# Moving the choice of the next image's tokens behind the present image's feed-forward, and splitting 165 kept tokens 83 + 82 instead of 128 + 37

## The chip, the cores and the metric

The kernel runs on one core of a Trainium2 chip. The metric is the device time of one execution in microseconds (us). Before the change it is 12924.97 us, the median of three runs (12904.25 to 12950.39). The profile is of one more execution, which took 12889.47 us.

A core has five engines, each working through its own queue of instructions: TensorE (PE in the profile: matrix products; PEld: its weight loads), VectorE (DVE), ScalarE (ACT), GpSimd (POOL), and SyncE (SP), which here only starts DMA transfers.

## The reference, cut to what matters

64 images of 256 x 256 pass a tokenizer of four Fourier layers. The 256 rows of its output and 77 text tokens make 333 tokens of width 256 for each image. One layer follows, image by image, and the change lies in it:

```
h = concat([tokenizer(x), txt], axis=1)          # [64, 333, 256]
h = h + attention(layernorm(h))                  # one head, softmax over 333 tokens
z = layernorm(h)
weights = z @ wr + br                            # one number for each token
sel = the 165 tokens of largest weight, in order # k = 166 by top_k, the last one dropped
y = (gelu(z[sel] @ w1 + b1) @ w2 + b2) * weights[sel]
out = h + z;  out[sel] += y
```

All arithmetic is in float32.

## The kernel before, in words

The first three quarters of the time go to the tokenizer, whose order is written out by hand (a `manual_schedule` block) and which the change doesn't touch. The last stage, from about 9950 us on, handles the 64 images one after the other. Its program order is a loop over the images (L1038 to L1046), but the framework's scheduler decides at build time in which order each engine's queue gets the instructions: among those that are ready by its own estimate it prefers the one that comes first in the program. Once built, each queue is fixed, and semaphores make an instruction wait for what it needs.

Four functions make up an image's work.

- `image_rows(b)` (L809 to L838) makes the last tokenizer step. DVE forms two small products (L813, L817), PE multiplies them (L819), DVE copies the result (`y`, through L163), and PE starts a sum in the PSUM tile `hp` with it (L824). Then come eight pieces `ch` of 1 MB, loaded by SP (L829, five buffers), each with four matmuls (L831). Each of these matmuls appears twice in the profile, so a piece is 8 PE instructions and an image has 64. ACT moves the finished `hp` into `h` (L836), and SP loads the text rows (L837).
- `attention(h)` (L903 to L966) is a layer norm (`layer_norm`, L840: statistics L845 and L846 on DVE, root L848 on ACT, reciprocal L849, normalised rows `az` by L853), transposition by PE (L863) with copies of `azT`, the queries (L909), scores (L921), their maximum (L926) and exponential (L928), the values (L935), the transposed probabilities (L950), the product (L959) and the residual sum `h1` (L962). A second layer norm gives `z` (its tile is `fz`). At the end it called `select(z)`.
- `select(z)` (L867 to L901) finds the kept tokens. DVE takes the weight of each token (L875) and puts it on a diagonal (`dg`, L879), one such matrix for each group of 128, 128 and 77 tokens; PE turns the three into a row of all weights in every partition (L880); DVE moves it out (L882), and then counts by comparisons how many tokens beat each one (L889, L893, L895, L898). The count gives the factor `fw` (L899) and the 0/1 matrix `place` (L900), which maps tokens to kept places.
- `feed_forward(b, h1, z, fw, place)` (L970 to L1036) gathers the kept tokens by a product with `place` (L977, copied to `zs`), transposes `place` in two pieces for the way back (L988, copied to `back`), applies the two layers (L994, gelu on ACT at L998, L1005, bias L1009 to `yT`), transposes the result in the same two pieces (L1015, copied to `ys`), scatters it by a product (L1024, two pieces for each group of tokens), and adds it to the rest (L1027). SP stores the result in 17 transfers (L1032, L1036). POOL adds `z` to `h1` (L1020) and the output bias to `h` (L955).

`evict` (L157) copies alternate between DVE (L163) and ACT (L161).

In the loop, iteration `b` does `image_rows(b + 2)`, then `attention(b + 1)` with its `select`, then `feed_forward(b)`. So the choice for image `b + 1` stood ahead of the feed-forward of image `b`, whose own choice had been made one iteration earlier. In the built queues the PE order for one image was: L909, L921, L935, L950, L959 with one piece of L831 inside it, two pieces of L831, L880, L977, L988, L994, L1005, L1015, L1024, L819, L863, L824, five pieces of L831. In this order L880 and L977 are interleaved.

Of the kernel before, what the change touches and what calls it, by code (L numbers as in the profile page):

```python
# [25 lines left out]
KEPT = max(1, int(0.5 * TOK)) - 1  # L26
# [96 lines left out]
def tile_fno_fusion_transformer(ctx: ExitStack, tc: tile.TileContext, a, cst_d, grid_d, out):  # L123
    nc = tc.nc
    x = a["x"].rearrange("b x y o -> b x (y o)")
    B = x.shape[0]
# [30 lines left out]
    def evict(dst, src, act_every=3):  # L157

        flip[0] += 1
        if act_every and flip[0] % act_every == 0:  # L160
            nc.scalar.copy(dst, src)  # L161
        else:
            nc.vector.tensor_copy(dst, src)  # L163
# [642 lines left out]
    def psum():  # L806
        return pp.tile([128, 512], F32, name="pp")
# [32 lines left out]
    def layer_norm(h, name):  # L840
        mv = small.tile([128, 3, 2], F32, name=f"{name}mv")
        nc.vector.memset(mv, 1.0)
        for t in range(3):
            bs = small.tile([128, 6], F32, name=f"{name}bs")
            nc.vector.bn_stats(bs[:rows[t]], h[:rows[t], t, :])  # L845
            nc.vector.bn_aggr(mv[:rows[t], t, :], bs[:rows[t]])  # L846
        rs = small.tile([128, 3], F32, name=f"{name}rs")
        nc.scalar.activation(rs, mv[:, :, 1], AF.Sqrt, bias=epsc, scale=1.0)  # L848
        nc.vector.reciprocal(rs, rs)  # L849
        z = tp.tile([128, 3, D], F32, name=f"{name}z")  # L850
        for t in range(3):
            r = rows[t]
            nc.vector.tensor_scalar(  # L853
                z[:r, t, :], h[:r, t, :], mv[:r, t, 0:1], rs[:r, t:t + 1], ALU.subtract, ALU.mult
            )
        if name == "f":
            return z
        zT = tp.tile([128, 2, TOK], F32, name=f"{name}zT")
        for dh in range(2):
            ps = psum()  # L860
            for t in range(3):
                r = rows[t]
                nc.tensor.transpose(ps[:, toks[t]], z[:r, t, 128 * dh:128 * dh + 128], ID[:r, :r])  # L863
            evict(zT[:, dh, :], ps[:, :TOK], 2)
        return z, zT

    def select(z):  # L867


        wcol = small.tile([128, 3], F32, name="wcol")  # L870
        ps = psum()
        for t in range(3):
            r = rows[t]
            junk = tp.tile([128, TOK], F32, name="junk")
            nc.vector.scalar_tensor_tensor(  # L875
                junk[:r, :D], z[:r, t, :], 1.0, wrB[:r], ALU.mult, ALU.mult, accum_out=wcol[:r, t:t + 1]
            )
            dg = tp.tile([128, 128], F32, name="dg")
            nc.vector.tensor_scalar(dg[:r, :r], ID[:r, :r], wcol[:r, t:t + 1], None, ALU.mult)  # L879
            nc.tensor.matmul(ps[:, toks[t]], lhsT=ONES[:r], rhs=dg[:r, :r], start=True, stop=True)  # L880
        wrow = tp.tile([128, TOK], F32, name="wrow")
        nc.vector.tensor_scalar(wrow, ps[:, :TOK], brB, None, ALU.add)  # L882
        fw = small.tile([128, 3], F32, name="fw")
        place = tp.tile([128, 3, KEPT], F32, name="place")
        for t in range(3):
            r = rows[t]
            junk = tp.tile([128, TOK], F32, name="junk")
            wc = small.tile([128, 1], F32, name="wc")
            nc.vector.scalar_tensor_tensor(  # L889
                junk[:r, :r], wrow[:r, toks[t]], 1.0, ID[:r, :r], ALU.mult, ALU.mult, accum_out=wc[:r]  # L890
            )
            gt = small.tile([128, 1], F32, name="gt")
            nc.vector.tensor_scalar(junk[:r], wrow[:r], wc[:r], None, ALU.is_gt, ALU.add, accum_out=gt[:r])  # L893
            eq = small.tile([128, 1], F32, name="eq")
            nc.vector.scalar_tensor_tensor(  # L895
                junk[:r], wrow[:r], wc[:r], TRI[:r, t, :], ALU.is_equal, ALU.mult, accum_out=eq[:r]
            )
            nc.vector.tensor_add(gt[:r], gt[:r], eq[:r])  # L898
            nc.vector.tensor_scalar(fw[:r, t:t + 1], gt[:r], float(KEPT), wc[:r], ALU.is_lt, ALU.mult)  # L899
            nc.vector.tensor_scalar(place[:r, t, :], IOTA[:r], gt[:r], None, ALU.is_equal)  # L900
        return fw, place  # L901

    def attention(h):  # L903
        z, zT = layer_norm(h, "a")
        qT = tp.tile([128, 2, TOK], F32, name="qT")
        for eh in range(2):
            ps = psum()
            for dh in range(2):
                nc.tensor.matmul(  # L909
                    ps[:, :TOK], lhsT=wqk[:, dh, 128 * eh:128 * eh + 128], rhs=zT[:, dh, :],  # L910
                    start=dh == 0, stop=dh == 1,
                )
            nc.scalar.activation(qT[:, eh, :], ps[:, :TOK], AF.Identity, bias=bqk[:, eh:eh + 1], scale=1.0)
        v = tp.tile([128, 3, D + 2], F32, name="v")
        p_ = tp.tile([128, 3, TOK], F32, name="prob")
        sm = small.tile([128, 3], F32, name="sm")
        for t in range(3):
            r = rows[t]
            ps = psum()
            for eh in range(2):  # L920
                nc.tensor.matmul(  # L921
                    ps[:r, :TOK], lhsT=qT[:, eh, toks[t]], rhs=zT[:, eh, :], start=eh == 0, stop=eh == 1
                )
            scale = 1.0 / D ** 0.5
            mx = small.tile([128, 1], F32, name="mx")
            nc.vector.reduce_max(mx[:r], ps[:r, :TOK], axis=AX.X)  # L926
            nc.vector.tensor_scalar_mul(mx[:r], mx[:r], -scale)
            nc.scalar.activation(  # L928
                p_[:r, t, :], ps[:r, :TOK], AF.Exp, bias=mx[:r], scale=scale, accum_out=sm[:r, t:t + 1]
            )  # L930
        for t in range(3):
            r = rows[t]
            ps = psum()
            for dh in range(2):
                nc.tensor.matmul(  # L935
                    ps[:r, :D + 2], lhsT=zT[:, dh, toks[t]], rhs=wvE[:, dh, :], start=dh == 0, stop=dh == 1
                )
            nc.vector.tensor_add(v[:r, t, :], ps[:r, :D + 2], bvE[:r])
            nc.vector.reciprocal(sm[:r, t:t + 1], sm[:r, t:t + 1])

            for n in range(2):
                nz = small.tile([128, 1], F32, name="nz")
                nc.vector.tensor_scalar(nz[:r], v[:r, t, D + n:D + n + 1], 0.0, None, ALU.not_equal)
                nc.vector.tensor_mul(sm[:r, t:t + 1], sm[:r, t:t + 1], nz[:r])
        pT = tp.tile([128, 3, TOK], F32, name="probT")
        for jt in range(3):
            r = rows[jt]
            ps = psum()
            for t in range(3):
                nc.tensor.transpose(ps[:r, toks[t]], p_[:rows[t], t, toks[jt]], ID[:rows[t], :rows[t]])  # L950
            evict(pT[:r, jt, :], ps[:r, :TOK], 2)
        h1 = tp.tile([128, 3, D], F32, name="h1")
        for t in range(3):
            r = rows[t]
            nc.gpsimd.tensor_add(h[:r, t, :], h[:r, t, :], boB[:r])  # L955
            ps = psum()
            for jt in range(3):
                rj = rows[jt]
                nc.tensor.matmul(  # L959
                    ps[:r, :D], lhsT=pT[:rj, jt, toks[t]], rhs=v[:rj, jt, 0:D], start=jt == 0, stop=jt == 2  # L960
                )
            nc.vector.scalar_tensor_tensor(  # L962
                h1[:r, t, :], ps[:r, :D], sm[:r, t:t + 1], h[:r, t, :], ALU.mult, ALU.add
            )
        z = layer_norm(h1, "f")
        return (h1, z) + select(z)  # L966

    kept = [slice(0, 128), slice(128, KEPT)]

    def feed_forward(b, h1, z, fw, place):  # L970

# [65 lines left out]

    hs = {n: image_rows(n) for n in range(min(2, B))}  # L1038
    done = attention(hs.pop(0))
    for b in range(B):  # L1040
        now = done
        if b + 2 < B:
            hs[b + 2] = image_rows(b + 2)
        if b + 1 < B:
            done = attention(hs.pop(b + 1))
        feed_forward(b, *now)  # L1046


# [31 lines left out]
```

## Time and profile before

| | |
|---|---|
| runs | 12904.25, 12924.97, 12950.39 us |
| profiled execution | 12889.47 us, span 12887.7 us |
| busy share of the span | PE 89%, PEld 47%, DVE 68%, ACT 47%, POOL 9% |
| last stage (9950 to 12888 us) | 2938 us; PE busy 2657.59 us, DVE 1714.61, ACT 1040.41, POOL 322.02 |
| last stage, TensorE clock granted | 0.97 |
| last stage, DMA | 196 GB/s, share 0.53 |

A group line of the profile names line, engine, operation, the tile written and the tiles read, the shape (partitions x elements), the count, the busy time, the mean of one in ns, and after the second bar the time for which the engine was idle just before these instructions and what ended it. In the chain of waits each line is a start, a duration and the instruction or wait that the end of the program hung on at that moment. "PEclk" is the share of full clock that TensorE was granted. [...]durations of successive matmuls overlap; what one costs in a run is the distance of the starts.

### The profile page before, as it was taken

Reading aid. Unit: us, or ns where it says so; the run is one execution under the profiler, and the core shown is the slowest. Engines: PE = TensorE matmul, PEld = TensorE weight load, DVE = VectorE, ACT = ScalarE, POOL = GpSimd, SP = SyncE. Lnnn points to the kernel's source line nnn. Section 1 sums busy time; section 2 is a strip of 40 time slices with the busy share of each in tenths; the row PEclk is TensorE's granted clock in tenths of the full one; section 3 lists DMA queues with packets and bytes.
Section 4 is the critical chain, followed back from the end, with each engine's and each line's share of the span. In section 5 each row is a group of like instructions: output and inputs, shape, how many; then the busy total and the mean of one; then the engine's idle time right before and its main releaser. Section 6 shows DMA issues by size and latency. Waiting matters only on the chain.

```text
span 12887.7 us, 406626 instructions
## 1 busy us (share of the span) xinstructions
PE 11449.8 (89%) x182458; PEld 6025.9 (47%) x182458; DVE 8775.7 (68%) x10606; ACT 6088.1 (47%) x10114; POOL 1110.9 (9%) x1183
## 2 busy tenths in 40 slices
PE   7799999999699999999969999999996899999998
PEld 5344444444344444444434444444443566666666
DVE  2777777777677777777767777776775556665555
ACT  2455555555355555555545555555553333333333
POOL 2100000000200000000020000000002111111111
PEclk9899999999899999999989999999997999999999
DMA  4555555555888889899989998988898555555553
GB/s 116 199 202 200 202 204 200 202 203 201 288 344 345 349 347 353 346 353 352 352 295 349 352 352 346 349 346 345 343 348 281 193 202 209 207 197 197 200 206 138
DMA packets 571125, 3484.57 MB, mean 270 GB/s; under 512 B 78224, under 2 KB 129248, under 8 KB 172448
## 3 DMA queue, kind: packets, MB, share of 16 engines
q1 hardware_dynamic: 565376, 3454.84, 71.0%
q8 instruction: 1428, 23.40, 0.7%
q0 software_dynamic: 4000, 3.71, 0.1%
q14 instruction: 321, 2.63, 0.1%
HBM read 1761.32 MB, written 1696.92 MB: 268 GB/s over the span
## 4 chain that ended last, share of the span: by engine, by line
PE 69%; DVE 16%; issue 7%; DMA 4%; ACT 3%; POOL 1%; SPq 0%; DVEq 0%; ACTq 0%; POOLq 0%
PE ring L607 14%; PE ring L624 13%; PE ring L572 11%; PE ring L583 7%; PE ring L647 4%; PE hp L831 3%; DVE t L595 3%; DVE vo L591 2%; DVE zt L634 2%; PE pp L959 2%; PE pp L994 2%; PE pp L1024 2%; PE pp L921 2%; PE pp L935 1%; PE pp L909 1%
## 5 line engine op out<-in xcount | busy, mean ns | idle before, releaser
L614 ACT ACTIVATE ring<-ring 128x1024 f32<-128x1024 f32 x3072 | 3108.9, 1012 | 1194.7 <-PE ring L607 1159.3
L595 DVE STREAM_TRANSPOSE t<-vo 128x2048 f32<-128x2048 f32 x1536 | 3550.1, 2311 | 173.5 <-ACT vo L590 12.6
L607 PE MATMUL ring<-vo,w 32*32 32x512 f32 x49152 | 2849.6, 624 | 391.2 <-DVE zt L634 139.6
L590 ACT ACTIVATE vo<-ring 128x1024 f32<-128x1024 f32 x1536 | 1568.2, 1021 | 3012.4 <-PE ring L583 2363.1
L591 DVE TENSOR_SCALAR vo<-ring 128x1024 f32<-128x1024 f32 x1536 | 1858.2, 1210 | 612.1 <-PE ring L583 424.5
L624 PE MATMUL ring<-t,cst 32*32 32x512 f32 x49152 | 1862.7, 602 | 288.5 <-issue 288.5
L634 DVE STREAM_TRANSPOSE zt<-ring 128x1024 f32<-128x1024 f32 x384 | 712.0, 1926 | 1630.5 <-PE ring L624 1630.5
L607 PEld LDWEIGHTS ring<-vo,w 32*32 32x32 f32 x49152 | 761.8, 105 | 1899.6 <-ACT ring L614 482.3
L624 PEld LDWEIGHTS ring<-t,cst 32*32 32x32 f32 x49152 | 981.1, 103 | 1132.1 <-issue 674.5
L583 PE MATMUL ring<-vin,ws 32*32 32x512 f32 x32768 | 1240.2, 608 | 19.9 <-issue 17.4
L542 POOL TENSOR_TENSOR ams<-am,sk 48x512 f32<-48x512 f32 x384 | 486.9, 1268 | 8439.5 <-DMA am<-mix 8005.8
L647 PEld LDWEIGHTS ring<-cst,zt 128*128 128x128 f32 x4608 | 533.2, 193 | 174.9 <-ACT vo L590 162.6
L614 ACT ACTIVATION_READ_ACCUMULATOR ring<-ring 128x1 f32 x3072 | 584.2, 190 | 0.0
L647 PE MATMUL ring<-cst,zt 128*128 128x96 f32 x4608 | 565.3, 279 | 9.2 <-DVE zt L634 9.2
L831 PE MATMUL hp<-ch,win 128*32 128x512 f32 x4096 | 487.1, 604 | 5.1 <-DMA ch<-v 5.1
L553 PE MATMUL ring<-ams,cst 49*128 49x512 f32 (+1 forms) x1536 | 392.4, 620 | 59.5 <-POOL ams L542 49.1
L583 PEld LDWEIGHTS ring<-vin,ws 32*32 32x32 f32 x32768 | 253.4, 103 | 402.6 <-issue 369.7
L926 DVE TENSOR_REDUCE mx<-pp 128x1 f32<-128x333 f32 (+1 forms) x192 | 96.6, 503 | 457.4 <-PE pp L921 453.9
L1020 POOL TENSOR_TENSOR h<-h,fz 128x256 f32<-128x256 f32 (+1 forms) x192 | 182.5, 975 | 1886.6 <-DVE fz L853 1886.6
L1005 PE MATMUL pp<-g,w 128*128 128x165 f32 x2048 | 314.8, 306 | 9.2 <-ACT g L998 3.6
L994 PE MATMUL pp<-zs,w 128*128 128x165 f32 x2048 | 305.4, 307 | 3.3 <-DVE zs L163 3.3
L1005 PEld LDWEIGHTS pp<-g,w 128*128 128x128 f32 x2048 | 292.2, 189 | 24.4 <-ACT g L998 24.4
(955 smaller groups left out, 11982.8 us busy)
## 6 DMA issues: line engine op xcount, KB each, us to landing
v<-vo SPq DMA_DIRECT2D x1536, 1024.0 KB
vin<-v SPq DMA_DIRECT2D x1024, 1024.0 KB
ch<-v SPq DMA_DIRECT2D x512, 1024.0 KB
mix<-ob SPq DMA_DIRECT2D x192, 256.0 KB
am<-mix SPq DMA_DIRECT2D x384, 96.0 KB
xin<-in_x_dram SPq DMA_DIRECT2D x64, 256.0 KB
mv<-in_x_dram SPq DMA_DIRECT2D x256, 64.0 KB
out_dram<-o SPq DMA_DIRECT2D x1024, 16.0 KB
```

The source lines that it names most:

```text
L572: nc.tensor.matmul(ps[n][:, 256 * r:256 * r + 256], lhsT=y_[b][32 * n:32 * n + K, t // 4, q:q + 4, :].rearrange("p q c -> p (q c)"), rhs=m ...
L583: nc.tensor.matmul(ps[n][32 * j:32 * j + 32], lhsT=ws[32 * n:32 * n + 32], rhs=v[32 * n:32 * n + 32, 2 * j:2 * j + 2, :], start=False, sto ...
L590: nc.scalar.activation(of[:, 0:2], t2[0], AF.Relu)
L591: nc.vector.tensor_scalar(of[:, 2:4], t2[1], 0.0, None, ALU.max)
L595: nc.vector.transpose(t32[b, t // 2][:, :, 8 * (t % 2):8 * (t % 2) + 8, :].rearrange("p y s c -> p s y c"), o.rearrange("p s (y l) -> p s ...
L607: nc.tensor.matmul(ps[n][32 * j:32 * j + 32], lhsT=w4[i + 1][32 * n:32 * n + 32], rhs=o[32 * n:32 * n + 32, 2 * j:2 * j + 2, :], start=Tru ...
L614: nc.scalar.activation(t2[n], t2[n], AF.Square, accum_out=acc[:, at:at + 1])
L624: nc.tensor.matmul(ps[n][32 * j:32 * j + 32], lhsT=FYT[32 * n:32 * n + 32, k, :], rhs=t32[b, j][32 * n:32 * n + 32, k].rearrange("p s c -> ...
L634: nc.vector.transpose(zt[:, h].rearrange("p k c -> p c k"), t2[h].rearrange("p n (s c) -> p c (n s)", c=C),)
L647: nc.tensor.matmul(ps[:, 0, 96 * g:96 * g + 96], lhsT=zt[:, h, k0:k0 + 4, :].rearrange("p k c -> p (k c)"), rhs=FX[:, h, 48 * r:48 * r + 9 ...
L831: nc.tensor.matmul(hp[32 * g:32 * g + 32], lhsT=win[:, 7 - t:39 - t], rhs=ch[:, g], start=False, stop=t == 7, skip_group_check=True,)
L1005: nc.tensor.matmul(ps[:, :KEPT], lhsT=w2[:, hb, 128 * dh:128 * dh + 128], rhs=g[:, hb, :], start=hb == 0, stop=hb == HID // 128 - 1,)
```

## The change

The call of `select` leaves `attention` and is put behind `feed_forward(b)` in the loop, so that the choice for image `b + 1` comes after the feed-forward of image `b` in program order, and ahead of `image_rows(b + 3)` and `attention(b + 2)`. For the first image it follows `attention(0)`. The two pieces in which kept tokens are transposed and scattered are 83 and 82 long instead of 128 and 37.

```diff
         z = layer_norm(h1, "f")
-        return (h1, z) + select(z)
+        return h1, z
 
-    kept = [slice(0, 128), slice(128, KEPT)]
+    kept = [slice(0, (KEPT + 1) // 2), slice((KEPT + 1) // 2, KEPT)]
...
     done = attention(hs.pop(0))
+    done += select(done[1])
     for b in range(B):
         now = done
         if b + 2 < B:
             hs[b + 2] = image_rows(b + 2)
         if b + 1 < B:
             done = attention(hs.pop(b + 1))
         feed_forward(b, *now)
+        if b + 1 < B:
+            done += select(done[1])
```

Built, the changed program has these queues in the last stage (the order of instructions is fixed before any run; line numbers are those of the kernel before, which differ by three or less). On PE, L880 stands after L1024, in one group of two and one later, around L819; L977 follows L959. The pieces of L831 are no longer in three runs for each image: in the first nine images there are three to five runs, and from then on six or seven, between the instructions of L959, L977, L988, L994 and L1005, with the last two or three pieces after L824. On ACT the eight gelus (L998) of an image stand together, and the root for the next image's `az` comes after the copy of `ys`; table loads ahead of L998 fall from 124 to 66. On DVE, L813 and L817 for a later image now stand ahead of the copy of `ys` or of L1027. The layer norm rows `az` of the next image stand ahead of the comparisons of `select` in 36 images, and behind nearly all of them (behind the last L895) in 26 images: every second one from the eleventh on.

## The prediction

> **What bounds the kernel now.** I read the busy times by stage first, then the waits of PE in the last stage, then the chain of waits through one image, then PE's and DVE's timelines of that image. The stages:
>
> ```profile
> 0.00:9950.00 9950.00, 8792.24 (x167162) 4253.60 (x167162) 7061.08 (x4408) 5047.66 (x8073) 788.91 (x799) 0.96 0.78 292
> 9950.00:12888.00 2938.00, 2657.59 (x15296) 1772.29 (x15296) 1714.61 (x6199) 1040.41 (x2041) 322.02 (x384) 0.97 0.53 196
> ```
>
> The columns are the stretch, its length, the busy times of PE, PEld, DVE, ACT and POOL, PE's clock, the DMA share and GB/s. Only the second line can change. PE is busy for 90% of it (DVE 58%), so it is PE's queue, and the 280 us in which PE stands, that count. PE's waits in this stage:
>
> ```profile
> PE pp L880 <- DVE dg L879: 197.3, 64, 7.6
> PE pp L1024 <- DVE ys L163: 25.3, 62, 0.4
> PE pp L1015 <- ACT yT L1009: 17.4, 64, 0.3
> ...
> PE pp L1005 <- ACT g L998: 3.6, 24, 0.2
> ```
>
> One wait dominates: `select`'s first matmul waits for its diagonal, 197.3 us over 64 images. The chain of waits through one image shows why:
>
> ```profile
> 11000.10 1.94 PE pp L959 x8
> ...
> 11002.14 0.49 DVE h L962
> 11002.66 0.43 DVE fbs L845
> ...
> 11003.87 1.46 DVE fz L853 x3
> 11005.33 0.69 DVE junk L875 x4
> 11006.02 1.35 DVE dg L879 x2
> ...
> 11007.42 0.49 PE pp L880 x2
> ```
>
> From the last product of attention to L880 runs a ladder over DVE and ACT (second layer norm, weights, diagonal), 5.4 us long. PE fills part with two pieces of L831 and stands for 2.94 us (each image repeats after 44.32 us). The feed-forward behind it (L977) needs none of this: its own choice is an iteration old.
>
> [...]the clock is halved. Here even the 2.94 us gap sometimes does it:
>
> ```profile
> 10555.07:10561.89 6.82, 5.93 (x24) 5.74 (x25) 5.67 (x23) 0.30 (x1) 1.34 (x2) 0.50 0.70 265
> 10602.85:10606.27 3.42, 3.42 (x13) 3.25 (x14) 2.28 (x8) 0.00 (x0) 0.39 (x1) 0.50 1.03 400
> ```
>
> That pair comes once in eight images (358 us) and makes two of them 46.85 and 45.65 us long instead of 44.32: 3.9 us. [...]L853 on 77 rows takes 808 ns beside POOL's L955, on 128 rows 409 ns.[...]
>
> **The change part by part**, on the profiled execution (12889.47 us). Which queue gets what is read from the built program; durations from the trace.
>
> 1. *L880 leaves the place between L959 and L977.* L977 can start when L959 ends. The 197.3 us go, but for a few at the first and last image: -193. What is late next is in 3 to 5.
>
> 2. *The gelus stay together.* Before, the next image's root (L848) parted them with two table loads of 1.28 us. 58 loads go, 74 us of ACT. PE waited only 3.6 us for gelu, because L1005 had other blocks to multiply: -3.
>
> 3. *L831 is cut into more runs.* Each run of these 32-column matmuls has a price, from PE's timeline:
>
> ```profile
> 10993.09 2.78 PE L935 MATMUL pp<-wvE,azT 128*128 128x258 f32 x12
> ...
> 10996.68 2.43 PE L959 MATMUL pp<-v,probT 128*128 128x256 f32 x10
> 10999.04 1.07 PE L831 MATMUL hp<-ch,win 128*32 128x512 f32 x8
> 11000.03 2.00 PE L959 MATMUL pp<-v,probT 77*128 77x256 f32 x8
> 11001.96 0.64 PE L831 MATMUL hp<-ch,win 128*32 128x512 f32 x4
> ```
>
> By the starts, one piece alone takes 0.99 us; in the run of five it took 4.43 / 5 = 0.89, so 0.10 more. L959's 18 instructions take 2.36 + 1.93 = 4.29 us; at L935's undisturbed pace (2.61 / 12 = 0.2175) they would take 3.92. That 0.37 belongs to two entries and two exits, some 0.2 a run. So a run costs about 0.3 to 0.33. From 3 runs to 6 or 7 in 52 images, and one more in the first nine: (52 x 3.5 + 9) x 0.33 = +63. Between the narrower products of the feed-forward the edges may hide; the run's own lengthening is the least. Bounds +19 (0.10) and +63; I take +63, as every edge in the trace pays.
>
> 4. *The comparisons of `select` now stand on DVE behind the feed-forward; in 26 images ahead of the next `az`*, whose transposition (L863) PE needs next. From the last L1024: L880 (twice two instructions) and L819 take PE 1.2 us, the copy `y` 0.4, so L882 starts at 1.7. From L882 to the end of the last L895 the trace has 11008.75 to 13.83, less 0.24 for a copy between: 4.8, so 6.5. The reciprocal (0.18), three L853 (1.47 beside POOL) and the L898 to L900 between them (0.5): 8.7. The last L863 and the copy of `azT`: 9.5. Until then PE has L880 1.0, L819 0.55, L824 1.06, two pieces of L831 1.85, L863 0.73: 5.2. It waits 4.3, and 0.4 more for `y` at L824 and for a second `azT` copy: 26 x 4.7 = +122. Before, `az` was done 7 us before L1024 ended. Bounds 3[...] and 6: +78 to +156.
>
> In the other 36 images `az` comes first. There the comparisons lie beside L909 and L921 and end before L926 is due (4.2 us after L909 starts): nothing. `place` itself is due at L977, over 15 us later: nothing.
>
> 5. *In 27 of these 36, `ys` is late.* DVE has the `az` statistics, L813 and L817 ahead of the copy `ys`, and they wait for L836, that is for the last piece of L831. After it: 0.15 and 0.69 (L836), then L845 three times at 0.32, L813 1.12, L846 0.1, L817 1.83 by the distances of starts: 4.9. PE meanwhile has 20 to 22 instructions of L1005 at 0.14, 3.0, and then 0.85 to `ys` (11019.92 to 11020.77): 3.85. Late by 1.0: 27 x 1.0 = +27, bounds 0 and +55.
>
> 6. *The clock.* From the last L831 to L909 there are some 5.5 us with only 0.7 of transpositions in them, which can halve the clock oftener than 2.94 us did. The shortest half-clock record is 3.41 us[...]: I take 0.45, so 12 of 26 at 3.9 us, +45, and the old eight pairs go, -31: +14. Bounds -31 and +70.
>
> 7. *83 + 82.* The same number of instructions, moving the same columns: L988 of 128 and of 37 columns takes 290 and 289 ns, L1024 with 128 and 37 rows 431 and 429; copies of 37 and 128 rows cost by their 333 columns (ACT 431 ns). 0, bounds ±4 for the weight loads (151 and 123 ns, hidden under the matmuls).
>
> 8. *DMA.* L829 and the 17 stores keep their order around L1027. After the stores five buffers are free and 5 MB arrive in about 13 us (11032 to 11045 at some 420 GB/s), while the first of these pieces is due 20 us after L1024. With `ch` waits of 5.1 us in the whole stage: 0, bounds 0 and +15.
>
> Sum: -193 - 3 + 63 + 122 + 27 + 14 = **+30 us**: 12919 on the profiled execution, which lies 0.3% under the median; on the median **12955**. A measurement here can tell about 0.3% (39 us) from no change.
>
> **The rivals.**
>
> - *Slower, by a half-clock trap.* At L863 PE nearly stands for 5.5 us in every second image. If each of these gaps, rather than a third to a half, halves the clock, 26 x 3.9 = 101 replaces the old 31: +70 instead of +14; with the wait at 5.3 instead of 4.7, +16 more: 13027. It decides from the point where the clock record shows 0.5 after most of these gaps. For it: 2.94 us were enough at times. Against: eight in sixty.
> - *Faster, since the new waits are smaller than read.* Edges of L831 hidden beside products of 165 columns (+19), a wait of 3.5 at L863 (+91), `ys` in time (+5), no half clock from the old gap (-10): -193 - 3 + 19 + 91 + 5 - 10 = -91, so 12834. For it: DVE and ACT have 40% and more of slack. Against: the edges are in every case of the trace, and the order on DVE is fixed.
> - *It doesn't do what it says.* That L880 still stands in PE's way could only be if the queue were not as built; the wait would merely move to L977 (for `place`). That is 15 us early: no chance given.
>
> **How the numbers follow.** The forecast's case has a chance of 0.46; by its own spread (bounds of 3 to 5 mostly, about ±30) 0.29 of that is within 0.3%, 0.15 above, 0.02 below. The slower rival has 0.30, of which 0.27 above. The faster rival has 0.24, of which 0.19 below. Slower 0.42, within 0.3% 0.37, faster 0.21. The range leaves a tenth on each side: from 12865, short of the faster rival's own time, to 13035, past the slower rival's. The likeliest case alone holds 12925 to 12990.
>
> **What would show it.** Step 1: no wait L880 <- DVE `dg` of more than some us in all, and L977 straight behind L959. Step 3: PE's starts around single pieces of L831 between L994 and L1005 show 0.3 us a run. Step 4: a wait of PE at L863 for `az` and L909 for `azT` of 110 to 130 us in all, in every second image, with L895 just before `az` on DVE. Step 5: L1024 <- `ys` at about 50 us instead of 25.3. Step 6: the clock at 0.5 behind these gaps. The forecast is wrong if L863 hardly waits, or if the images alternate by 44 and 49 us rather than 44 to 46.

## The result, and the profile after

The changed kernel takes 12849.98 us (median of 4 runs, 12845.12 to 12878.92); the kernel before, on the same chip, 12933.66 (4 runs, 12904.25 to 12950.39). The ratio is 0.9942 (95% interval 0.9918 to 0.9967): faster by 0.6%, where the forecast was 0.2% slower with a range that began at 12865 us. The profiled execution took 12849.86 us (span 12848.1), 39.6 less than that of before. So about half of the gain between the medians is seen between the two profiles; the profile of before lay 44 us under the median of these runs, that of after on its median. Two executions in the experiments, one of the kernel before (18084 us, clock 0.78) and one of e5 (22392 us, clock 0.51), were in a slow state and are left out of every comparison.

The last stage by its busy times (stretch, length, PE, PEld, DVE, ACT, POOL, PE's clock, DMA share, GB/s), and PE's longest waits in it (total us, times, longest):

```profile
9950.00:12849.00 2899.00, 2693.06 (x15296) 1785.46 (x15296) 1705.51 (x6199) 984.68 (x1984) 326.11 (x384) 0.96 0.55 198
```

```profile
PE pp L863 <- DVE az L853: 78.5, 52, 2.7
PE pp L1024 <- DVE ys L163: 46.0, 61, 1.6
PE pp L909 <- ACT azT L161: 19.6, 41, 0.5
PE pp L1015 <- ACT yT L1009: 18.1, 64, 1.0
PE pp L880 <- DVE dg L879: 9.8, 13, 7.6
```

The wait at L880 has gone from 197.3 to 9.8 us, and new waits have come at L863, L909 and for `ys`. All of PE's waits over 0.15 us together fall by 70 us, from 265.6 to 195.3, yet PE is busy for 36 us longer, at a clock of 0.96 instead of 0.97. PE's timeline shows the cost of the single pieces of L831 between the products of the feed-forward (start, duration, group, idle time before):

```profile
11005.88 1.06 PE L831 MATMUL hp<-ch,win 128*32 128x512 f32 x8
11006.88 2.51 PE L994 MATMUL pp<-zs,w 128*128 128x165 f32 x16
11009.32 1.06 PE L831 MATMUL hp<-ch,win 128*32 128x512 f32 x8
```

Sixteen L994 take 2.44 us from start to start of the next group, 0.15 each with the edge, against 0.14 in the unbroken run of before (4.54 / 32); each piece takes 1.00, where a piece of a run of five takes 0.89 on average.

What the forecast did not have is L1024. Before:

```profile
11021.25 3.75 PE L1024 MATMUL pp<-ys,back 128*128 128x256 f32 x12 [0.41 <-DVE ys L163]
11024.94 0.62 PE L819 MATMUL pp<-cstt,a 48*32 48x256 f32 x2
```

and after:

```profile
10970.34 2.87 PE L1024 MATMUL pp<-ys,back 83*128 83x256 f32 x12 [0.40 <-DVE ys L163]
10973.04 0.61 PE L880 MATMUL pp<-dg,cst 128*128 128x128 f32 x4
```

From its start to that of the next group the same twelve instructions take 3.69 us before and 2.70 after; over all images at full clock 3.681 and 2.705. That is 0.976 us an image, 62.5 us in all.

### The profile page after: what moved, and what is told of

It is laid out like the page before. It is cut to its first block, busy times and chain, and to the rows that moved or that the text cites. A ratio compares the mean times of both kernels' runs of the same rounds, so it can differ in the third digit from the quotient of the medians.

```text
span 12848.1 us, 406325 instructions
## 1 busy us (share of the span) xinstructions
PE 11486.4 (89%) x182458; PEld 6038.9 (47%) x182458; DVE 8768.3 (68%) x10606; ACT 6032.7 (47%) x10057; POOL 1115.6 (9%) x1183
## 4 chain that ended last, share of the span: by engine, by line
PE 70%; DVE 17%; issue 7%; DMA 4%; ACT 1%; POOL 1%; SPq 0%; DVEq 0%; ACTq 0%; POOLq 0%
PE ring L607 14%; PE ring L624 13%; PE ring L572 11%; PE ring L583 7%; PE ring L647 4%; PE hp L831 3%; DVE t L595 3%; DVE vo L591 3%; PE pp L994 2%; DVE zt L634 2%; PE pp L959 2%; PE pp L921 2%; PE pp L909 2%; PE pp L1005 1%; PE pp L935 1%
## 5 line engine op out<-in xcount | busy, mean ns | idle before, releaser
L583 PE MATMUL ring<-vin,ws 32*32 32x512 f32 x32768 | 1235.7, 606 | 25.1 <-issue 20.7
L831 PE MATMUL hp<-ch,win 128*32 128x512 f32 x4096 | 533.6, 615 | 5.0 <-DMA ch<-v 5.0
L845 DVE BATCH_NORM_STATS2 abs<-h 128x6 f32<-128x256 f32 (+1 forms) x192 | 75.9, 402 | 439.3 <-ACT h L836 419.1
L994 PEld LDWEIGHTS pp<-zs,w 128*128 128x128 f32 x2048 | 291.2, 190 | 99.2 <-issue 68.8
L994 PE MATMUL pp<-zs,w 128*128 128x165 f32 x2048 | 332.1, 310 | 0.0
L1005 PEld LDWEIGHTS pp<-g,w 128*128 128x128 f32 x2048 | 292.5, 189 | 73.6 <-issue 68.8
L1005 PE MATMUL pp<-g,w 128*128 128x165 f32 x2048 | 321.5, 307 | 0.1
```

The costliest lines, as they stand in the source:

```text
L583: nc.tensor.matmul(ps[n][32 * j:32 * j + 32], lhsT=ws[32 * n:32 * n + 32], rhs=v[32 * n:32 * n + 32, 2 * j:2 * j + 2, :], start=False, sto ...
L831: nc.tensor.matmul(hp[32 * g:32 * g + 32], lhsT=win[:, 7 - t:39 - t], rhs=ch[:, g], start=False, stop=t == 7, skip_group_check=True,)
L994: nc.tensor.matmul(ps[:, :KEPT], lhsT=w1[:, dh, 128 * hb:128 * hb + 128], rhs=zs[:, dh, :], start=dh == 0, stop=dh == 1,)
```

## The experiments

Each ratio is to the kernel before, measured beside it on the same chip; its median was then 12899 to 12928 us. "Half-clock time" is the sum of the stretches with 0.5 in the clock record of the profiled execution that begin after 9950 us; nearly the same number follows from the stage's PEclk, as 2 x (1 - PEclk) x length. An "undisturbed image" is the distance from one image's first L909 to the next where no such stretch lies between. Where a kernel has lines inserted, its line numbers behind them are one to three higher: L1025 to L1027 are then the scatter product that is L1024 before.

### One part at a time: e1 to e4

**e1: before, with pieces of 83 and 82.**

```diff
-    kept = [slice(0, 128), slice(128, KEPT)]
+    kept = [slice(0, (KEPT + 1) // 2), slice((KEPT + 1) // 2, KEPT)]
```

> The kernel before with the pieces of 83 and 82 alone; the choice of tokens stays where it was. Theory A (the pieces brought the gain: in L1024, weights of 128 rows and of 37 rows alternated, and each change between them kept the next weight load from being done ahead): L1024 takes 2.70 us for an image instead of 3.68, so 62 us faster, ratio 0.995, and PE's wait at L880 stays at about 197 us. Theory B (the move brought the gain, as the split costs and saves nothing): ratio 1.000, L1024 at 3.68 us.

Measured: 12916.62 us, 1.0003 (0.9993 to 1.0012). The ratio is that of theory B, and yet theory B does not hold: L1024 takes 2.797 us an image here, 0.884 less than before, and no gain comes of it.

**e2: the kernel after, with pieces of 128 and 37** (the same line, the other way).

> The choice of tokens moved behind the feed-forward, the pieces left at 128 and 37. Theory A: L1024 at 3.68 us for an image; the move alone costs +23 us by the two profiles (12848.1 - 12887.7 + 62.5), ratio 1.002, or up to 20 us less than before if the execution profiled before was a low one: 0.998 to 1.003. Theory B: the whole measured gain, ratio 0.994.

Measured: 13048.33 us, 1.0101 (1.0084 to 1.0117): slower by 1%. Both theories miss.

**e3: before, with pieces of 101 and 64** (`slice(0, 101), slice(101, KEPT)`).

> The kernel before with pieces of 101 and 64. Theory A1 ([...]the change of kind costs): L1024 stays near 3.68 us, ratio 1.000. Theory A2 (the 37-row operand was dear by its being short or by the unevenness of the two): L1024 falls by more than half of the 0.98 us, ratio about 0.997.

Measured: 12925.22 us, 1.0009 (0.9997 to 1.002). L1024 takes 3.681 us, exactly as with 128 and 37: with 64 rows in the smaller piece it is as dear as with 37.

**e4: before, 128 and 37, with the loop over the pieces outermost in L1024**, so that the kind of piece changes once instead of five times. It needs three PSUM tiles at a time.

```diff
-            ps = psum()
-            for c, k in enumerate(kept):
-                n = k.stop - k.start
+        pss = [psum() for t in range(3)]
+        for c, k in enumerate(kept):
+            n = k.stop - k.start
+            for t in range(3):
+                r = rows[t]
                 nc.tensor.matmul(
...
+        for t in range(3):
+            r = rows[t]
```

> The kernel before, pieces 128 and 37, but in the scatter product all three token groups of the first piece come first and then all three of the second (three PSUM tiles open at once)[...]. Theory A (alternation costs): L1024 at about 2.8 us, ratio 0.995 to 0.996; DVE's L1027 come later by about 1.3 us, and what of that PE sees is taken off. Theory that 37-row matmuls are dear in themselves: 3.68 us less at most the 0.1 of a few changes, ratio 1.000.

Measured: 12938.8 us, 1.0023 (1.0016 to 1.003). The group takes 2.98 us instead of 3.68, and the kernel is still no faster.

So the matmuls became cheaper in e1 and e4, and the time did not become shorter. The last stage of e1, and in it a stretch behind the gap at L880:

```profile
9950.00:12933.00 2983.00, 2688.37 (x15328) 1888.69 (x15328) 1722.24 (x6208) 1043.22 (x2043) 322.23 (x384) 0.94 0.52 195
...
11167.71:11174.54 6.83, 6.83 (x27) 6.59 (x28) 5.67 (x28) 0.85 (x3) 0.39 (x1) 0.50 0.57 211
```

The clock of the stage is 0.94; before it was 0.97. After the gap of 2.94 us at L880, which is the same as before, PE runs 6.83 us at half clock. Half-clock time is 177 us before, 344 in e1, 259 in e3, 380 in e4, 248 after, and 607 in e2:

```profile
9950.00:13054.00 3104.00, 2914.20 (x15305) 1805.55 (x15304) 1714.45 (x6203) 984.51 (x1985) 325.04 (x384) 0.90 0.50 186
```

From this comes **theory C**: each part of the change is worth what the starts of its instructions say, and the rest is half-clock time, set off by gaps of PE. **Rival D**: the split gains only together with the late choice, for a reason in the order of the work.

The clock changes on a fixed grid: in the traces of before and after, all its edges in this stage, up to the end of the last record, lie whole multiples of 3.4133 us apart, to 1 ns, and the shortest half-clock record is 3.413 us; the 6.83 us of e1 above are two such steps. A step of this grid is called a window below. By theory C, whether a gap halves the clock depends on where in a window it falls, and so on the length of an image. The image of before lasts 44.313 us, 12.98 windows. Its gap moves back by only 0.06 us an image in the grid. While its start lies between 1.38 and 1.7 us into a window, the clock stays full; at 1.34 to 1.37 and at 0.4 us, the next window is at half clock. This pair comes once in eight images. In e1 an image without one would last 43.43 us, 12.7 windows, and every gap is caught: the lengths repeat as 46.42, 45.07, 45.04 us, 136.53 in all, which is 40.0 windows.

### The choice at other places, so that the gap is smaller: e5 to e9

**e5: the choice in the middle of the feed-forward, behind L988, pieces of 128 and 37. e6: the same with 83 and 82.** `feed_forward` gets one more argument, called behind the copies of `back`:

```diff
-    def feed_forward(b, h1, z, fw, place):
+    def feed_forward(b, h1, z, fw, place, then=None):
...
             evict(back[:n, c, :], ps[:n, :TOK], 2)
+        nxt = then() if then else None
...
-        feed_forward(b, *now)
-        if b + 1 < B:
-            done += select(done[1])
+        nxt = feed_forward(b, *now, (lambda: select(done[1])) if b + 1 < B else None)
+        if b + 1 < B:
+            done += nxt
```

> The kernel before, with the choice for image b+1 called in the middle of the feed-forward of image b (behind the copies of back, L988, in program order) and pieces 128 and 37. Built, L880 stands behind L988, az stands ahead of ys on DVE in every image, and L831 lies in four runs an image. Theory C (each part of the change is worth what the durations say, and the rest is half-clock windows of PE, about 0.48 us lost for each us of clock 0.5 in the last stage): no gap of PE above 2 us is left, so the wait at L880 goes (-193), one more run of L831 (+21), and the 177 us at half clock in the last stage go down to under 30 (-70): 0.981 of before, and the clock record nearly free of 0.5 after 10400 us. Rival D (moving the choice away from the place behind L959 costs something by itself, as the slower run with the move alone says): not below 0.995.

> The same with pieces of 83 and 82, queues otherwise identical. Theory C: with no half-clock windows to give it back, the twelve L1024 at 2.7 instead of 3.7 us an image show in the time in full: 62 us (0.48%) under the run with 128 and 37 of the same call, 0.976 of before. Rival D (the split gains only together with the late choice): equal to that run within 0.1%.

Measured: e5 12929.16 us, 1.0015 (1.0004 to 1.0026); e6 12814.87 us, 0.9925 (0.9906 to 0.9944). Both levels are missed: the wait at L880 is still 153 and 162 us, since the copies of `zs` and `back` now stand on DVE inside the chain that leads to `dg`, and gaps of 2.0 to 2.25 us stay in each image. But the two differ by 114 us, against Rival D. Theory C's 57 us of L1024 (64 x 0.884) are half of it. Half-clock time is 359 us in e5 and 238 in e6, and 0.45 us for each of these 121 us (the part on the length of the image has this number) is the other half. e5 also shows that no long gap is needed:

```profile
10802.89:10806.31 3.42, 2.74 (x11) 1.36 (x10) 1.97 (x6) 0.70 (x2) 2.26 (x3) 1.00 0.00 0
10806.31:10809.72 3.41, 3.41 (x8) 0.84 (x6) 0.96 (x2) 0.00 (x0) 0.00 (x0) 0.50 0.11 21
```

In the first window, around L1016 and L1025, PE stands for only 0.27 and 0.41 us; the clock is halved in the next one, and stays so for three windows.

**e7: the choice behind the copies of `zs`, ahead of L988, pieces of 83 and 82. e9: the same with 128 and 37.** As e5, with the call two lines higher.

> The choice called behind the copies of zs (L977) and ahead of L988, pieces 83 and 82. Built, PE has L959, six L977, two pieces of L831 and then L880: the ladder over DVE takes 5.4 us, the products before L880 some 3.7, so a gap of 1.5 to 2 us stays in each image, short of the 2.05 us of idle time inside one clock window that the traces show ahead of a half-clock window. Theory C: gap 1.7 x 64 = 109 us instead of 197 and few half-clock windows: 0.98 of before. If a gap of this size is enough for half clock: 0.99 and records of 0.5 after each gap.

> The kernel of e7 (choice called behind the copies of zs) with pieces of 128 and 37; queues otherwise identical. Its gap of 1.36 us an image is the smallest so far and halved the clock in only every third image, so this is the cleanest pair for the pieces. Theory C: L1025 at 3.7 instead of 2.7 us an image, images without half clock at 42.55 instead of 41.57 us; with about as many half-clock windows, 62 us above e7 (0.988 to 0.990 of before), 30 either way if the windows differ. Rival D (the pieces gain only in the kernel after): equal to e7 within 0.1% (0.984).

Measured: e7 12709.35 us, 0.9839 (0.9818 to 0.986); e9 12805.33 us, 0.9919 (0.9898 to 0.9939). PE in e7:

```profile
11310.11 1.92 PE L831 MATMUL hp<-ch,win 128*32 128x512 f32 x16
11313.40 1.08 PE L880 MATMUL pp<-dg,cst 128*128 128x128 f32 x4 [1.36 <-DVE dg L879]
```

Two pieces of L831 lie together again, and the gap is 1.36 us. The expectation's 2.05 us of idle time in a window is no border: half clock follows a window with 1.69 us in the kernel after (12335.63 to 12339.04), and does not follow one with 2.02 us in the kernel before (11224.08 to 11227.49). The number is near theory C's 0.98. An undisturbed image lasts 41.57 us; with one half-clock window of 3.41 us in it, 43.24: such a window costs 1.67 us. In e9 the undisturbed image lasts 42.44, 0.87 more, which is L1024's 0.884. The two differ by 96 us: 57 from L1024, and some 42 (0.45 x 93) from half-clock time of 226 against 133 us. Rival D falls: the split is worth its 57 us in a third order too.

**e8: the kernel after, with the choice called from inside the next attention, behind its first layer norm**, so that `az` stands ahead of the comparisons in all images.

```diff
-    def attention(h):
+    def attention(h, then=None):
         z, zT = layer_norm(h, "a")
+        if then is not None:
+            then()
```

> The kernel after, with the choice called from inside the next attention, behind its first layer norm, so that az stands ahead of the comparisons on DVE in all images (in the kernel after it stands behind them in 26). Theory C: the waits at L863, L909 and L824 (100 us) go, the half-clock windows that follow them go too (up to -90), and two runs of L831 fewer in 52 images (-30): 0.977 of before. If the half-clock windows of the kernel after do not come from these waits: -100 only, 0.986.

Measured: 12754.07 us, 0.9874 (0.9856 to 0.9892), against 0.9942 for the kernel after. The wait at L863 is gone; half-clock time goes from 248 to 157 us. New waits of 41 us (for `prob`) and 24 us (for `probT`) take the place of some of it, and those for `yT` (L1015) grow from 18 to 36 us. So theory C's 0.977 is missed. The number is that of the other expectation, 0.986, but not for its reason, since 91 us of half-clock time did go.

### The length of the image: e10, e11, e13, e14

These keep the order of before and its gap of 2.94 us, and change only how long an image lasts. **e10** adds one needless matmul of 32 columns among L988, **e11** two of 128, **e14** (on e1) four of 124:

```diff
+            if c == 0:
+                for i in range(2):
+                    nc.tensor.matmul(ps[:, 336:336 + 128], lhsT=ID, rhs=place[:, 0, 0:128], start=True, stop=True)
             evict(back[:n, c, :], ps[:n, :TOK], 2)
```

**e13** widens L959 to 258 columns and half of L994 to 167.

> The kernel before with one needless matmul of 32 columns more in each image, between the transpositions L988; the order is otherwise the same. It adds some 0.06 us of PE work an image, 4 us in all. Theory C, in its sharper form: the clock is granted in windows of 3.413 us on a fixed grid; the image of before lasts 44.315 us, 0.057 short of 13 windows, so the gap at L880 (2.94 us) drifts through the grid by 0.057 an image and is caught by a half-clock window once in eight images. With 0.06 us more the period is 13 windows, the drift all but stops, and the gap stays where it does no harm: half-clock time in the last stage from 177 us to under 100, and the program with more work 10 to 30 us faster (0.998). If the grid plays no part: 4 us slower and as many half-clock records as before (1.000).

> The same with two needless matmuls of 128 columns, about 0.45 us of work an image, 29 us in all. Theory C: the period is then 13.11 windows, the gap moves by 0.4 us an image and is caught every two or three images: the half-clock time in the last stage rises from 177 us to 250 to 350, and the time by 29 + 35 to 80 us (1.005 to 1.008). If the grid plays no part: 29 us (1.002) and the same half-clock time.

> The kernel before with two more columns in each L959 (258 instead of 256) and in half of L994 (167 instead of 165); results the same, order the same. By 0.85 ns a column that is 0.057 us more PE work an image, 3.7 us in all. Grid theory: the undisturbed image goes from 44.313 to 44.37 us, 13 windows of 3.4133, so that the gap at L880 stands still on the grid once it is in its harmless place: half-clock time in the last stage from 177 us to under 120 and the time 15 to 35 us shorter (0.9975 to 0.999), with more work. If the grid plays no part: 1.0003, and 177 us as before.

> The kernel before with pieces 83 and 82 (e1) and four needless matmuls of 124 columns in each image between the transpositions L988, 0.94 us by the cost of the two in e11: 60 us in all. Grid theory: the undisturbed image goes from 43.43 us (12.7 windows) to 44.37 (13 windows), the half-clock time in the last stage from 344 us to under 180, so the 60 us of work cost nothing: not slower than e1 (which was 1.0003 of before), 0.997 to 1.001. If the grid plays no part: 1.005.

Measured: e10 12963.07 us, 1.0044 (1.0031 to 1.0057). The small matmul cost 0.19 us an image instead of 0.06, so the gap did not stand still; 12 us of work made the kernel 64 us slower, with 307 us at half clock.

e11: 13095.49 us, 1.0146 (1.0123 to 1.017): 31 us of work (0.485 an image) cost 197 us, with 591 us at half clock. Its images lock to 47.78 us for a while, then to 51.23, and back: 14.0 and 15.0 windows.

e13: 12919.71 us, 1.0001 (0.9991 to 1.0011), with 210 us at half clock; the undisturbed image became 44.465 us, 0.15 longer instead of 0.06 (L935 in the trace of before takes 0.2175 us for 258 columns, 0.84 ns a column), so it does not decide.

e14: 12985.38 us, 1.0042 (1.0025 to 1.0058). Here the sharper form of theory C, that an image of 13 windows is harmless, falls: the image had the length that was meant (43.43 + 0.93), and yet the lengths repeat as 45.81, 46.85, 47.29, 139.95 in all or 41.0 windows, with half clock in each. The length alone does not fix the cycle, since e11 has two; that where the gap enters decides is an estimate. A gain by more work was not shown.

What stands is the sum. For the eight kernels with the order of before:

| kernel | PE work against before, us | half-clock time, us | span, us | span less work |
|---|---|---|---|---|
| before | 0 | 177 | 12887.7 | 12888 |
| e13 | +10 | 210 | 12930.5 | 12921 |
| e3 | +2 | 259 | 12924.5 | 12923 |
| e10 | +12 | 307 | 12968.1 | 12956 |
| e1 | -57 | 344 | 12933.1 | 12990 |
| e4 | -45 | 380 | 12949.5 | 12994 |
| e14 | +3 | 419 | 12994.2 | 12991 |
| e11 | +31 | 591 | 13112.2 | 13081 |

The work is 64 times the change of the group's starts (L1024 for e1 and e4, L988 with the added matmuls for e10, e11 and e14) or of the undisturbed image (e3, e13). A straight line through the last column is 12817 + 0.45 x half-clock time, and no kernel lies more than 18 us off it. Those 18 us are e1's, and its profile has one wait of 20.0 us at the start of the stage, for a weight that is still being loaded (L771), which that of before lacks; e13 has one of 18.9. The six kernels with the order of e7 (e7, e9 and e15 to e18 below), less the 57 us of L1024 in e9 and e18, give a slope of 0.54 in the same way, within 8 us. So about half of the half-clock time is lost. "No gain from the split" is -57 us of work and +75 us (0.45 x 167) of clock.

### What it is about the pieces: e15 to e18

All four are e7 with other pieces, `slice(0, n), slice(n, KEPT)`.

> The kernel of e7 with pieces of 96 and 69. If what costs L1024 time is that successive matmuls use a different number of groups of 32 rows (128 and 37: four and two; 101 and 64: four and two; 83 and 82: three and three), 96 and 69 are three and three: 2.8 us an image for the group, image 41.57 us, 0.984 as in e7. If it is the difference of the lengths: 3.2 to 3.7 us, image 42 to 42.4.

> The same with 97 and 68, four groups and three: with the theory of groups 3.7 us an image for L1025 and an undisturbed image of 42.44, though each piece is only one row longer or shorter than in e15. If it is the difference of the lengths: as e15.

> The kernel of e7 with pieces of 100 and 65. If what costs is that the second piece has 64 rows or fewer while the first has more, so that TensorE changes between two kinds of weights at each of the six steps, this is the last fast pair: 2.80 us for L1025, 0.984 of before. If the cost grows with the distance in another way: between 2.8 and 3.7 us.

> The same with 101 and 64, one row moved. If the border lies at 64 rows: 3.68 us for L1026, an undisturbed image 0.88 us longer and 56 us more work in all, so 0.989 to 0.992 of before as with 128 and 37 (e9). If not: as e17.

| pieces | L1025, us an image | time, us | ratio (interval) |
|---|---|---|---|
| 83 + 82 (e7) | 2.797 | 12709.35 | 0.9839 (0.9818 to 0.986) |
| 96 + 69 (e15) | 2.796 | 12702.38 | 0.9837 (0.9822 to 0.9853) |
| 97 + 68 (e16) | 2.796 | 12699.81 | 0.9831 (0.9816 to 0.9846) |
| 100 + 65 (e17) | 2.796 | 12702.04 | 0.9838 (0.982 to 0.9857) |
| 101 + 64 (e18) | 3.680 | 12833.56 | 0.9939 (0.9925 to 0.9954) |
| 128 + 37 (e9) | 3.681 | 12805.33 | 0.9919 (0.9898 to 0.9939) |

It is neither that the lengths are equal nor how many groups of 32 rows they fill: 97 and 68 are as fast as 96 and 69. One row moved from 65 to 64 costs 0.88 us an image. The border is at 64 rows. e18 is 131 us over e17: 57 us are the pieces, and 279 us at half clock against 129 cost some 67 more (0.45 x 149), so it misses its 0.989 to 0.992.

What changes inside TensorE at this border, no run shows. The traces give the price of a change from a piece on one side of it to one on the other. With pieces on both sides of 64, the six steps of L1024 alternate: five changes between the first and the last of the twelve starts, which lie 3.375 us apart instead of 2.490, so 0.177 us a change. e4 has one change there, and 2.676: 0.186.

The weight loads (PEld) show where the time goes. Before, ahead of the second pair:

```profile
11021.25 0.30 PEld L1024 LDWEIGHTS pp<-ys,back 128*128 128x128 f32 x2 [0.67 <-DVE ys L163]
11021.88 0.29 PEld L1024 LDWEIGHTS pp<-ys,back 37*128 37x128 f32 x2 [0.33 <-issue]
```

and after, all twelve:

```profile
10970.33 2.42 PEld L1024 LDWEIGHTS pp<-ys,back 83*128 83x128 f32 x12 [0.66 <-DVE ys L163]
```

After, from the third on, each load begins when the matmul ahead of its own begins, some 0.22 us early. Before, PEld stands for 0.33 us at each change, and the load begins only together with its matmul. By the starts, the step into a change takes 0.31 us and the step behind it 0.32 (0.28 where the weights have 77 columns), against 0.22 undisturbed: about 0.09 and 0.10. This is what theory A of e1 supposed.

The step from the last L1024 to L819, whose weights have 48 rows and 32 columns, takes 0.31 us behind a piece of 37 rows (before, e4) as behind one of 82 (e1, e7); the step to L880 in the kernel after takes 0.215. This is why L1024 took 2.797 us in e1 and 2.705 in the kernel after.

The groups by form, of e16 and of e18, show the same in the means (in ns, behind the busy time):

```profile
L1025 PE MATMUL pp<-ys,back 97*128 97x256 f32 x212 | 68.6, 405 | 21.6 <-DVE ys L163 21.6
L1025 PE MATMUL pp<-ys,back 68*128 68x256 f32 x212 | 63.2, 379 | 0.0
```

```profile
L1025 PE MATMUL pp<-ys,back 64*128 64x256 f32 x204 | 73.4, 441 | 0.0
L1025 PE MATMUL pp<-ys,back 101*128 101x256 f32 x204 | 71.3, 431 | 20.8 <-DVE ys L163 20.8
```

431 and 441 ns here, 431 and 428 before: both forms of an alternating pair have long records, so comparing one with the other shows no difference. The 379 ns of the second form of the fast pair show it; the 405 of the first hold the one long record behind the wait for `ys`.

### The best version found

**e12** tried to improve on e7: the choice behind the first copy of `back`, with the copies of `zs` and `back` on ACT.

> The best version in sight: as e7, but the choice called behind the first copy of back, and the copies of zs and back on ACT, so that DVE's ladder from the last L959 to L880 has no copy in it (5.4 instead of 5.7 us) and PE has three transpositions L988 more to do in it. Expected by the distances: gap 0.7 us instead of 1.36 (-40 us), fewer half-clock windows (-30), another run of L831 (+21): 0.980 of before. If windows are halved by the ends of the feed-forward rather than by this gap, they stay as many as in e7: 0.983.

Measured: 12782.51 us, 0.9901 (0.9882 to 0.992). The gap is 1.83 us instead of the 0.7 expected, and half-clock time 218 us: a miss. The copies on ACT lie ahead of the root L848 in its queue; that they lengthen the chain to `dg` was not tried. So e7 and its like with 96, 97 and 100 stay the best, 12700 to 12709 us, 1.6 to 1.7% under before and some 1.1% under the kernel after.

## Why the prediction was wrong

It failed by its step 7, "83 + 82 ... 0, bounds ±4": the split took 62.5 us off L1024. In part it failed by the way from the profile to the median. On the two profiled executions:

| step | forecast, us | measured, us |
|---|---|---|
| 1, L880 | -193 | -187.5 |
| 2, gelu | -3 | -3.6 (the wait L1005 for `g` is gone) |
| 3, runs of L831 | +63 | +64 (195 more runs x 0.33) |
| 4, `az` behind the comparisons | +122 | +99 (L863 78.5, L909 19, L824 some 2) |
| 5, `ys` | +27 | +20.7 |
| 6, clock | +14 | +32 (71 us more at half clock x 0.45) |
| 7, pieces | 0 | -62.5 |
| 8, DMA | 0 | 0 (`ch` 5.0 instead of 5.1) |
| not forecast: L977 in the last image, L994 in the first | | +0.5 (+3.8 - 3.3) |
| sum | +30 | -37, against -39.6 between the profiles |

**Step 1** was right: L977 follows L959 without idle time in the steady images. **Step 3** was right in its price: a run costs 0.33 us: 0.09 at the entry, 0.10 at the exit, and 0.14 in the pieces, since a piece alone takes 0.996 where each further piece of a run adds 0.858. (The prediction read 0.10 for the last by the mean of a run of five.) **Steps 4 and 5** were right in place and mechanism (in the 26 images of step 4, DVE begins `az` within 0.12 us of the end of the last L895), and their forecasts somewhat too large.

**Step 6** had the right sign. Half clock does follow the gaps at L863, in the profile of the kernel after at 10977 us:

```profile
10976.98:10980.50 3.52, 0.86 (x9) 0.16 (x2) 3.52 (x21) 0.00 (x0) 0.07 (x1) 1.00 0.46 88
10980.50:10987.30 6.80, 6.19 (x15) 3.47 (x15) 1.74 (x5) 0.98 (x2) 2.43 (x3) 0.50 0.95 390
```

This happened within 5.5 us of the start of all 26 gaps there (1.44 to 2.68 us long), not in 0.45 of the cases, which was the author's estimate; it cost less than the "trap" rival allowed, since the first ten images lost half-clock time that they had before. +32 is within the bounds given (-31 and +70), but in part by luck, as e2 shows below: the prediction tied half clock to single gaps, and had no term for the length of the image.

**Step 7** was taken from durations: 431 and 429 ns for pieces of 128 and 37 rows, so no difference in rows. But these are the two halves of an alternation, and both pay for it. The prediction itself had said that in a run the distance of the starts is what counts, and had priced the edges of L831 from it; it did not measure L1024's starts (0.307 us apart, where the 258 columns of L935 need 0.2175), and counted instructions and columns, not changes of kind. With -62.5 in the place of 0 the sum is -32.5, a forecast of 0.25% faster.

The rest of the miss: the forecast put the profile of before 35 us under the median and added this to the result as well. The profiled execution of after lies on its median. Single runs of before spread from 12871 to 12965 us over all experiments; what moves them was not settled, though a wait like those at L771 can be part of it.

The gain is not spread evenly. Between the two profiles the first ten images go from 463.1 to 416.4 us, -46.7; there `az` is not yet behind the comparisons, and 27 us of half clock go. The other 53 go from 2373.5 to 2387.5, +14.0: from the eleventh image on, the new waits, the edges and the clock take back all that L880 and L1024 give. There the new waits and the edges came much as forecast.

For the move alone the forecast of +30 was wrong. The profile of e2 is 167 us over that of before. PE's waits over 0.15 us fall by 89 us there, the 195 runs of L831 add 64, and 429 us more at half clock cost some 193 by the slope of the table: +168. So with pieces of 128 and 37 the clock cost 193 us and not 14, though the waits at L863 are shorter there (62 us instead of 78.5), and the slower rival's 13027 would have been nearer. The split then gained 198 us between the medians of e2 and of the kernel after, 62.5 of them in L1024; the rest goes with 358 us less at half clock. The slope comes from another order; no run of e2's order without half clock was made.

Left open: by what rule half clock follows a gap. A share of idle time alone does not give it: in e7 the same gap of 1.36 us, wholly inside a window, halved the clock in some images and not in others. What told them apart was the place. Of the 53 such gaps, the 18 that began in the first 0.31 us or the last 0.25 us of a window were followed by half clock, and the 35 that began between 1.21 and 3.11 us were not.

## What to carry to other kernels

Price a group of matmuls by the distance of the starts, against a group of the same columns that does not alternate; float32 matmuls of 256 columns with over 64 and with up to 64 rows of weights in turn cost about 0.18 us at each change here, and two pieces should be cut so that both lie on one side. Where PE has a gap in every round of a loop, the clock can take back what a small change gives (+75 us against -57 in e1) or double it (114 us for 57 from e5 to e6): compare the half-clock time of two traces before judging a change of 1%, and shorten the gap first. A change whose parts gain nothing alone, as in e1 and e2, can still gain as a whole.

## What was unexpected in the hardware

- In the pairs tried, the number of rows of a matmul's weights matters only as being over 64 or not: 65 and 82 rows beside 100 and 83 are alike (2.796 and 2.797 us), 64 beside 101 costs 3.680. At a change the weight load is not done ahead, and PEld stands for 0.33 us.
- Half clock followed gaps of 1.36 us in part of the images, and in e5 a window with waits of only 0.27 and 0.41 us; about half of the time at half clock is lost (slopes of 0.45 and 0.54).
- The images of these loops with a gap lock to the clock's grid of 3.4133 us: periods of 14.0 and 15.0 windows for one image (e11), 40.0 for three (e1), 41.0 for three (e14), 54.0 for four (e10). Adding 0.19 us of work to each image cost 1.0 us each (e10).
